# A macaron layer: scanning in place in PSUM, expert parameters in one tensor of two halves, and parts of setup and plan moved into the first units

## The chip, the cores and the metric

The kernel runs on one core of one Trainium2 chip, in float32. The metric is the time of one execution on the device in microseconds. A core has five engines with instruction queues of their own: PE (matrix products), DVE (vector), ACT (activation functions), POOL (which also issues the indirect gathers and scatters) and SP (which issues the direct transfers). Each engine works through its queue in order; semaphores order them among one another. The products of PE land in PSUM, eight banks of 128 x 512 floats.

## The reference

```
x = x + 0.5 * moe(layernorm(x))
x = x + block(layernorm(x))
x = x + 0.5 * moe(layernorm(x))
```

There are 4096 tokens (2 sequences of 2048) of 256 features. `moe` gives each token its two best of 8 experts by a softmax gate. Each expert takes at most 640 tokens of first and 640 of second choices, in token order; what comes later is dropped. Expert: `relu(x @ W1 + b1) @ W2 + b2` with 1024 hidden features, times the gate's probability.

`block` is a selective scan followed by a small MLP, each behind an RMS norm. Its core, for 512 channels and 16 states:

```
u  = silu(causal_conv4(x @ in_proj))         # and a gate z
dt = softplus(low_rank(u) @ dt_proj + b)
h[t] = h[t-1] * exp(dt[t] * A) + dt[t] * u[t] * B[t]     # per channel and state
y[t] = sum over states (h[t] * C[t]) + D * u[t]
out  = (y * silu(z)) @ out_proj
```

Then comes `x + relu(norm(x) @ c_fc)^2 @ c_proj`. The inputs are seeded random numbers; the gate's and the experts' biases are small random numbers.

## The kernel before, in words

**Routing.** `setup` makes constants and loads the block's weights; on DVE it builds `half`, sixteen diagonal matrices `taps` (a convolution tap on the diagonal, so that PE does the convolution) and four `skip`, and scales `w_out`. `moe1` then routes the 32 tiles of 128 tokens in groups of 4, 4, 8, 8 and 8 (`route`): layer norm, gate logits, top two, position of each token in its expert's list. `store_list` puts the lists into DRAM.

**Plan.** The tokens of an expert are cut into units of 256 rows. `plan` (L643) works out on DVE, from the counts, which expert and which rows each possible unit has, for 39 units at once; `fetches` and `index` turn this into row numbers for the gathers. In the first MoE the units of the first half of the tokens come first and then those of the second half, so `plan` gets 16 columns, 8 experts for each half.

**First MoE.** `run_units` runs 22 units (`NU_A`) through `units` (L762): for unit u, ids of u+5 are gathered, `hidden` multiplies by W1 (PE, ACT), the rows of u+1 are transposed, `finish` multiplies by W2, adds the bias on DVE and issues two scatter-adds into `acc` in DRAM on POOL, and then the rows and parameters of u+3 are gathered into one of three buffers. A unit whose expert's parameters are in that buffer already gets a row number out of range, so that its gather moves nothing; the instruction remains. An expert's parameters are two gathers: 8,224 bytes a partition from `expert_in` (W1, b1) and 9,216 from `expert_out` (W2, b2). `then` is a table of functions that are called at the start of a unit: `begin_rest` at unit 18 asks for the ids and parameters of the first spread unit.

**The block.** The tokens are cut into eight chunks of 512. The scan's loop (`recurrence`) has 512 slots: 8 chunks x 4 channel blocks x 16 states. In a slot POOL makes `db` = dt·u·B, ACT makes `dA` = exp(dt·A) into PSUM (`decay`), DVE runs the scan along the 512 tokens into another PSUM bank `h`, ACT copies the last column as the state (`st`), DVE multiplies by C into `hc`, and PE adds `hc` up in `y_ps`. The pools `dA` and `h` have two banks each, `ps` and `yps` too. In the loop `scan(k)` and its `st` copy come ahead of `decay(k + 2)`:

```
            if k < len(order):
                scan(k)
                decay(k + 2)
            if k:
                output(k - 1)
            drive(k + 3)
```

**What is placed between the slots.** Everything else of the block, and 21 more units of the two MoEs, is cut into steps that the class `Side` puts between the slots when the program is built. Ten "b" units (`NU_B`) belong to the first MoE (second half of the tokens), eleven "c" units (`NU_C`) to the second (first half); `spread_units` builds both, with one parameter buffer in two parts, `wa` and `wb`. `chunk_front` prepares a chunk (norm, projection, convolution, `dt`, B and C), `chunk_tail` finishes it (output projection, MLP, and the routing for the second MoE). `Side` keeps a book of each engine's time. A slot adds `OWN` to it (DVE 1.95, ACT 0.88, POOL 1.27 us), a step adds its own cost, and a step is placed when its engines are not further ahead of the slot than `BEHIND` allows. If the loop needs a result that is not placed yet (`side.until`: for example `dt` of the next chunk, or the previous chunk's output before `gate`), the steps up to it are all placed at once at that slot. Which engine runs what in which order is thus fixed by this book, whose times are not measured during the run.

**Second MoE.** During the block, the lists are planned a second time (`plan_half` after four chunks, `plan_rest` after the last); then 21 units (`NU_D`) run as in the first MoE, added to `out`.

Of the kernel before, what the change touches and what calls it, by code (L numbers as in the profile page):

```python
# [18 lines left out]
P = 128  # L19
# [23 lines left out]
W_2 = W_B1 + NF  # L43
W_B2 = W_2 + NF * D
WW = W_B2 + D

# [29 lines left out]
class Side:  # L76
# [6 lines left out]
    OWN = {"dve": 1.95, "act": 0.88, "pe": 0.0, "pool": 1.27}  # L83
# [101 lines left out]
class Feed:  # L185


    def __init__(self, kernel, todo, data, pool, pre="", nids=8, nrows=4):
        self.nc, self.pool, self.pre = kernel.nc, pool, pre
        self.expert = kernel.ins["expert_in"], kernel.ins["expert_out"]  # L190
        self.idx, _, self.widx = todo
        self.lists, self.rows, _ = data
        self.nids, self.nrows = nids, nrows
        self.ids, self.xb = {}, {}
# [26 lines left out]
    def params_of(self, u, to):  # L221

        n = to.shape[1]
        parts = [to] if n < WW else [to[:, :W_2], to[:, W_2:]]
        for a in parts:
            src = self.expert[a.shape[1] != W_2]
            self.gather(a, src, self.widx[:, u : u + 1], E * P - 1)


class Kernel:  # L230
# [6 lines left out]
    def setup(self):  # L237
# [4 lines left out]
        self.wa = self.keep.tile([P, W_2], F32, tag="wa", name="wa")  # L242
        self.wb = self.keep.tile([P, WW - W_2], F32, tag="wb", name="wb")
        dp = self.ctx.enter_context(self.tc.tile_pool(name="scratch", bufs=1, space=DRAM))

        def const(shape, name, dtype=F32):
            return cp.tile(shape, dtype, tag=name, name=name)

        self.ident = const([P, P], "ident")
        make_identity(nc, self.ident)  # L250
        self.ones = const([P, P], "ones")
        nc.gpsimd.memset(self.ones, 1.0)

        self.before = const([P, P], "before")
        nc.gpsimd.affine_select(
            out=self.before, in_=self.ones, pattern=[[1, P]], compare_op=ALU.is_gt,
# [32 lines left out]
        self.before_b, self.ones_b = const([P, P], "before_b", BF16), const([P, P], "ones_b", BF16)  # L289
        nc.vector.tensor_copy(self.before_b, self.before)  # L290
        nc.vector.tensor_copy(self.ones_b, self.ones)
# [24 lines left out]
        nc.sync.dma_start(out=self.gb, in_=ins["gate_b"].partition_broadcast(P))  # L316
        def weights(name, src, k, n):
            t = const([P, k, n], name)
            nc.sync.dma_start(out=t, in_=ins[src].rearrange("(k p) n -> p k n", p=P))
            return t  # L320
# [23 lines left out]
        for c in range(NC):  # L344
# [7 lines left out]
        a_log = const([P, NC, DS], "a_log")  # L352
        nc.sync.dma_start(out=a_log, in_=ins["A_log"].rearrange("(c p) s -> p c s", p=P))
        a_exp = const([P, NC, DS], "a_exp")
        nc.scalar.activation(a_exp, a_log, AF.Exp)
        self.A = const([P, NC, DS], "A")
        nc.vector.tensor_scalar_mul(self.A, a_exp, -1.0)

        sizes = (NT, NT, NT // 2)
        self.rows = [
            dp.tile([n + 1, RW], F32, tag=f"rows{i}", name="rows") for i, n in enumerate(sizes)
        ]
        self.lists = [dp.tile([NULL + 1, 1], I32, tag=f"list{i}", name="lists") for i in range(3)]
        with self.tc.tile_pool(name="once", bufs=1) as once:
            row = once.tile([1, RW], F32, tag="none", name="none")
            nc.gpsimd.memset(row, 0.0)
            for t, n in zip(self.rows, sizes):
                nc.sync.dma_start(out=t[n:, :], in_=row)  # L370
            for i, n in enumerate((NT, NT // 2, NT)):
                none = once.tile([1, 1], I32, tag=f"none{i}", name="none")
                nc.gpsimd.memset(none, n)
                nc.sync.dma_start(out=self.lists[i][NULL:, :], in_=none)
        self.acc = dp.tile([NT, D], F32, tag="acc", name="acc")

# [266 lines left out]
    def plan(self, t, M, kept, half, nu, off, size=MU):  # L643
# [6 lines left out]
        V = nu.shape[1]  # L650
        WV, WE, WB = [P, M, V], [P, M, E], [P, M, UB]
        cu, cx, cb = t("cu", [P, V]), t("cx", [P, V]), t("cb", [P, V])
        v.tensor_tensor_scan(cu, self.ones[:, :V], nu, 0.0, ALU.mult, ALU.add)
# [11 lines left out]
        if V > E:  # L665
            ie = t("ie", WE)
            v.tensor_tensor(ie, inn[:, :, :E], inn[:, :, E:], ALU.add)
            inn = ie
# [48 lines left out]
    def fetches(self, t, name, eu, nwb, known=0):  # L717
# [3 lines left out]
        same, at, widx = t("same", [P, n]), t("at2", [P, n]), t(name, [P, n], I32)  # L721
# [4 lines left out]
        v.scalar_tensor_tensor(at, eu, float(P), self.part[:, :n], ALU.mult, ALU.add)  # L726
        v.scalar_tensor_tensor(widx, same, SKIP, at, ALU.mult, ALU.add)
        return widx
# [9 lines left out]
    def first_expert(self, pool):  # L738

        w = pool.tile([P, WW], F32, tag="w0", name="w0")  # L740
        self.nc.sync.dma_start(out=w[:, :W_2], in_=self.ins["expert_in"][:P, :])
        self.nc.sync.dma_start(out=w[:, W_2:], in_=self.ins["expert_out"][:P, :])
        return w
# [4 lines left out]
    def parts(self, *w):  # L748

        a, b = w[0][:, :W_2], w[-1][:, -(WW - W_2) :]  # L750
        return (
            a[:, :W_B1].rearrange("p (k f) -> p k f", k=ND), a[:, W_B1:],
            b[:, : W_B2 - W_2].rearrange("p (f d) -> p f d", f=NF), b[:, W_B2 - W_2 :],
        )
# [93 lines left out]
    def bank(self, lone):  # L848

        if not lone:  # L850
            return self.mm, "mm"
        self.lent += 1
        self.spare = self.spare[1:] + self.spare[:1]
        return self.spare[-1]

    def spread_units(self, feed, m0, acc, last, pool, name, slots, known):
# [4 lines left out]
        wa, wb = self.wa, self.wb  # L861
        w1, b1, w2, b2 = self.parts(wa, wb)
        if not known:
# [3 lines left out]
            feed.params_of(0, wa)  # L867
# [3 lines left out]
            feed.params_of(0, wb)  # L871
# [33 lines left out]
        for u, slot in enumerate(slots):  # L905
# [25 lines left out]
            if u + 1 < n:  # L931
                yield Need(pool=1.0, sets=(name + "wa", u + 1), late=9.0)
                feed.params_of(u + 1, wa)
# [13 lines left out]
            if u + 1 < n:  # L947
                yield Need(pool=1.0, sets=(name + "wb", u + 1), late=9.0)
                feed.params_of(u + 1, wb)

    def scratch(self, pool):
        def t(name, shape, dtype=F32):
            return pool.tile(shape, dtype, tag=f"p_{name}", name=name)

        return t
# [11 lines left out]
    def moe1(self):  # L967
# [4 lines left out]
        with ExitStack() as ctx:  # L972
# [27 lines left out]
            with tc.tile_pool(name="m1_lps", bufs=1, space=PSUM) as ps:  # L1000
# [4 lines left out]
            tot, off = t("tot", [P, K2, E]), t("off", [P, K2 * E])  # L1005
            v.tensor_tensor(tot[:, 0, :], half[:, :E], half[:, E:], ALU.add)
            v.tensor_tensor(tot[:, 1, :], kept[:, :E], kept[:, E:], ALU.add)
            nu = self.need(t, tot.rearrange("p c e -> p (c e)"), "nu")
            v.tensor_tensor(nu[:, E:], nu[:, E:], nu[:, :E], ALU.subtract)
            v.tensor_scalar_mul(off[:, :E], nu[:, :E], 0.0)  # L1010
            v.tensor_copy(off[:, E:], nu[:, :E])
            at, m0, eu, cu, _ = yield_from(self.plan(t, MU, kept, half, nu, off))


            over, o2, ok = t("over", [P, 1]), t("o2", [P, 1]), t("ok", [P, 1])
            v.tensor_scalar_add(over, cu[:, E - 1 : E], -float(NU_A))
            v.tensor_scalar_add(o2, cu[:, K2 * E - 1 :], -float(NU_A + NU_B))
            v.tensor_tensor(over, over, o2, ALU.max)
            v.tensor_scalar_max(over, over, 0.0)
            v.tensor_scalar(ok, over, 0.0, None, ALU.is_equal)  # L1020
            more = t("more_i", [P, 1], I32)
            v.tensor_copy(more, over)
            todo = self.index(t, "idx", at), m0, self.fetches(t, "widx", eu, NWB, 1)
            rest = slice(NU_A, NU_A + NU_B)
            m0b = keep("m0b", [P, NU_B, UB])
            v.tensor_copy(m0b, m0[:, rest, :])
            self.rest = (
                self.index(keep, "idxb", at[:, rest, :], ok), m0b,
                self.fetches(keep, "widxb", eu[:, rest], 1),
            )  # L1030
            data = self.lists[0], self.rows[0], self.acc
            self.feed_b = Feed(self, self.rest, data, self.keep, "e_", 4, 2)

            def begin_rest():
                self.feed_b.ids_of(0)
                self.feed_b.params_of(0, self.wa)
                self.feed_b.params_of(0, self.wb)

            then = {NU_A - 4: begin_rest, NU_A - 2: lambda: self.feed_b.rows_of(0)}
            self.run_units("m1", NU_A, todo, more, w, data, Feed(self, todo, data, pool), pool, then)  # L1040

# [17 lines left out]
    def plan_half(self, pool):  # L1059
# [14 lines left out]
        done, d2 = keep("done", [P, E]), t("d2", [P, E])  # L1074
        v.tensor_scalar(d2, cx, -1.0, float(NU_C), ALU.mult, ALU.add)
        v.tensor_scalar_max(d2, d2, 0.0)
        v.tensor_tensor(done, d2, nu, ALU.min)
# [3 lines left out]
        self.todo = self.index(keep, "idxc", at), m0c, self.fetches(keep, "widxc", eu, 1)  # L1081
# [251 lines left out]
    def recurrence(self, pools, chunks, side):  # L1333
# [36 lines left out]
        def decay(k):  # L1370
            if k < len(order):
                i, c, s = order[k]
                dA[k] = pools["dA"].tile(W1, F32, tag="dA", name="dA")
# [4 lines left out]
        def scan(k):  # L1378
            i, c, s = order[k]
            ch = chunks[i]  # L1380
            if k % (NC * DS) == 0:
                ch["state"] = stp.tile([P, NC, DS], F32, tag="st", name="st")
            h[k] = pools["h"].tile(W1, F32, tag="h", name="h")
            nc.vector.tensor_tensor_scan(  # L1384
                h[k], dA.pop(k), db.pop(k),
# [132 lines left out]
    def mamba(self):  # L1518
# [3 lines left out]
        with ExitStack() as ctx:  # L1522
# [5 lines left out]
            def aside(name, bufs):  # L1528
# [11 lines left out]
                "dA": pool("dA", 2, space=PSUM),  # L1540
                "h": pool("h", 2, space=PSUM),
# [3 lines left out]
            self.spare = [(pools["dA"], "dA"), (pools["h"], "h")]  # L1545
# [51 lines left out]
def layouts(inputs):  # L1597
# [9 lines left out]
        ff["b1"].reshape(E, NF, P).transpose(0, 2, 1),  # L1607
        ff["W2"].reshape(E, NF, P, D).transpose(0, 2, 1, 3).reshape(E, P, NF * D),
        np.broadcast_to(ff["b2"][:, None, :], (E, P, D)),
# [13 lines left out]
        "expert_in": np.concatenate(per_expert[:2], 2).reshape(E * P, W_2),  # L1623
        "expert_out": np.concatenate(per_expert[2:], 2).reshape(E * P, WW - W_2),
    }
# [18 lines left out]
```

## Time and profile before

| | |
|---|---|
| three runs | 2423.73, 2425.97, 2438.62 us (median 2425.97) |
| the profiled run | 2435.03 us, of it span 2433.3 us |
| PE busy | 2063.3 us, 85% |
| POOL busy | 1520.0 us, 62% |
| DVE busy | 1342.2 us, 55% |
| ACT busy | 1028.3 us, 42% |
| granted PE clock | 0.933 of full speed, mean |
| DMA | 328.51 MB, 135 GB/s mean |

The page's slices over the span (each of 40 is 60.8 us; a digit is the busy share in tenths) show the stages:

```profile
PE   5399999597988888896888887798997988699996
...
DVE  6611111115877868499788788785887823211111
ACT  3122222126546557455466663764663532122211
POOL 2366555429787768486577774885786742655553
```

Routing and plan are the first two slices, the first MoE the next six, with little DVE; then the block's front, the scan loop from about 572 to 1961 us, its tail, and the second MoE from about 2085 us. In the later views a row reads: line, engine, operation, out<-in by the program's names, shapes, count; busy time and mean duration in ns of one; the idle time ahead of it and what ended most of that. In a timeline a row begins with its start and its duration, and in brackets stands the idle time ahead of it.

### The profile page before, as it was taken

The page shows a single profiled execution, that of the slowest core. Times are in us where ns is not written, and L with a number is a line of the kernel's source. Part 1 is how long each engine was busy: PE and PEld are TensorE (multiplying, and loading weights), DVE is VectorE, ACT ScalarE, POOL GpSimd, SP SyncE. Part 2 cuts the span into 40 slices and gives each one's busy share as a digit, 9 for nine tenths or more (in the row PEclk, how much of TensorE's full clock was granted, in tenths as well). Part 3 has the DMA queues.
Part 4 walks back from the last instruction along what each step waited for, and adds up shares of the span by engine and source line. Part 5 has one row for each costly group of instructions (what it writes and reads, how often), then busy time and mean ns, then how long its engine had stood idle before and what let it go on. Part 6 is the DMA issues. An engine that isn't in the chain of part 4 may idle for free. (4 is left out here: it accounts for less than half of the span.)

```text
span 2433.3 us, 24340 instructions
## 1 busy us (share of the span) xinstructions
PE 2063.3 (85%) x7253; PEld 1317.4 (54%) x7253; DVE 1342.2 (55%) x2234; ACT 1028.3 (42%) x2335; POOL 1520.0 (62%) x1481
## 2 busy tenths in 40 slices
PE   5399999597988888896888887798997988699996
PEld 1188878453544454553433333354545566588875
DVE  6611111115877868499788788785887823211111
ACT  3122222126546557455466663764663532122211
POOL 2366555429787768486577774885786742655553
PEclk8699999798999999998999999999998999899998
DMA  7165556323655546364345354465455632455553
GB/s 248 58 207 147 173 162 210 81 62 84 169 136 128 120 128 162 90 169 113 97 113 147 100 143 98 124 190 126 99 132 137 150 117 67 118 165 178 177 180 98
DMA packets 163693, 328.51 MB, mean 135 GB/s; under 512 B 31795, under 2 KB 78748, under 8 KB 149212
## 3 DMA queue, kind: packets, MB, share of 16 engines
q1 hardware_dynamic: 116156, 173.92, 27.9%
q0 software_dynamic: 47392, 152.90, 21.7%
q8 instruction: 61, 1.00, 0.2%
q14 instruction: 84, 0.69, 0.1%
HBM read 316.35 MB, written 36.38 MB: 145 GB/s over the span
## 5 line engine op out<-in xcount | busy, mean ns | idle before, releaser
L1368 POOL TENSOR_TENSOR db<-dtu,bt 128x512 f32<-128x512 f32 x512 | 653.0, 1321 | 190.8 <-DVE h L1384 90.5
L1405 PE MATMUL y_ps<-hc,ident 128*128 128x512 f32 x1024 | 546.7, 636 | 120.7 <-DVE hc L1394 119.5
L1384 DVE TENSOR_TENSOR_SCAN h<-dA,st,db 128x512 f32<-128x512 f32 x384 | 494.5, 1288 | 73.0 <-POOL db L1368 35.7
L1405 PEld LDWEIGHTS y_ps<-hc,ident 128*128 128x128 f32 x1024 | 186.0, 197 | 369.3 <-DVE hc L1394 243.0
L794 ACT ACTIVATE h<-hp,w 128x256 f32<-128x256 f32 x344 | 144.4, 471 | 564.6 <-PE hp L836 473.5
L1374 ACT ACTIVATE dA<-dt,A 128x512 f32<-128x512 f32 x512 | 358.4, 700 | 2.5 <-POOL dt L1294 2.3
L1394 DVE TENSOR_TENSOR hc<-h,ct 128x512 f32<-128x512 f32 x512 | 344.7, 673 | 15.7 <-ACT st L1389 15.4
L836 PE MATMUL hp<-xbT,w 128*128 128x256 f32 x1376 | 308.0, 382 | 12.3 <-issue 11.5
L843 PE MATMUL yp<-w,h 128*128 128x256 f32 x1376 | 307.6, 382 | 0.0
L836 PEld LDWEIGHTS hp<-xbT,w 128*128 128x128 f32 x1376 | 264.0, 192 | 49.6 <-issue 11.9
L843 PEld LDWEIGHTS yp<-w,h 128*128 128x128 f32 x1376 | 260.9, 192 | 34.5
L1389 ACT COPY st<-h 128x1 f32<-128x1 f32 x512 | 81.2, 159 | 388.0 <-DVE h L1384 386.1
L779 DVE COPY xbT<-tp 128x512 f32<-128x512 f32 x43 | 29.7, 691 | 344.4 <-PE tp L775 344.4
L836 PE MATMUL e_hp<-e_xT,wa 128*128 128x256 f32 x672 | 180.8, 419 | 15.2 <-DVE h L1384 7.1
L1384 DVE TENSOR_TENSOR_SCAN h<-dA,db 128x512 f32<-128x512 f32 x128 | 157.2, 1228 | 51.0 <-POOL db L1368 38.9
L836 PEld LDWEIGHTS e_hp<-e_xT,wa 128*128 128x128 f32 x672 | 141.0, 213 | 70.6 <-issue 27.7
L805 DVE TENSOR_TENSOR y<-yp,w 128x256 f32<-128x256 f32 x86 | 36.5, 424 | 238.7 <-PE yp L843 238.7
L197 POOL DMA_INDIRECT xb<-rows,ids x128 | 134.3, 1049 | 37.6 <-issue 33.7
L843 PE MATMUL e_yp<-wb,e_h 128*128 128x256 f32 x672 | 152.9, 382 | 1.0 <-DVE xc L1213 1.0
L843 PEld LDWEIGHTS e_yp<-wb,e_h 128*128 128x128 f32 x672 | 128.6, 192 | 29.8 <-issue 10.8
L757 POOL DMA_INDIRECT acc<-y,ids x44 | 70.1, 1594 | 108.7 <-DMA acc<-y,ids 52.6
L757 POOL DMA_INDIRECT out<-y,ids x42 | 66.7, 1589 | 105.1 <-DMA out<-y,ids 65.7
(313 smaller groups left out, 2584.1 us busy)
## 6 DMA issues: line engine op xcount, KB each, us to landing
bt<-bc SPq DMA_DIRECT2D x256, 256.0 KB, 3.9
ct<-bc SPq DMA_DIRECT2D x256, 256.0 KB, 4.5
rows<-row SPq DMA_DIRECT2D x12, 512.0 KB, 4.7
x<-in_x SPq DMA_DIRECT2D x8, 512.0 KB, 4.5
acc<-x SPq DMA_DIRECT2D x8, 512.0 KB, 5.1
xt<-acc SPq DMA_DIRECT2D x8, 512.0 KB, 5.5
x<-acc SPq DMA_DIRECT2D x8, 512.0 KB, 4.8
out<-xt SPq DMA_DIRECT2D x8, 512.0 KB, 4.8
```

The costliest lines, as they stand in the source:

```text
L197: self.nc.gpsimd.indirect_dma_start(out=out, out_offset=None, in_=src, in_offset=bass.IndirectOffsetOnAxis(ap=idx, axis=0), bounds_check=l ...
L757: self.nc.gpsimd.indirect_dma_start(out=dst, out_offset=bass.IndirectOffsetOnAxis(ap=ids, axis=0), in_=y, in_offset=None, bounds_check=las ...
L794: nc.scalar.activation(h[:, f + q, :], hp[:, q, :], AF.Relu, bias=b1[:, f + q : f + q + 1])
L805: nc.vector.tensor_tensor(y[:, j, :], yp, b2, ALU.add)
L836: self.nc.tensor.matmul(hp[:, q, :], lhsT=w1[:, k, (f + q) * P : (f + q + 1) * P], rhs=xT[:, k, :], start=(k == 0), stop=(k == ND - 1),)
L843: self.nc.tensor.matmul(yp, lhsT=h[:, f, j * P : (j + 1) * P], rhs=w2[:, f, :], start=(f == 0), stop=(f == NF - 1),)
L1368: nc.gpsimd.tensor_tensor(db[k], chunks[i]["dtu"][c // PR][:, q, :], bt[n], ALU.mult)
L1374: nc.scalar.activation(dA[k], chunks[i]["dt"][c], AF.Exp, scale=self.A[:, c, s : s + 1])
L1384: nc.vector.tensor_tensor_scan(h[k], dA.pop(k), db.pop(k), chunks[i - 1]["state"][:, c, s : s + 1] if i % (T // TC) else 0.0, ALU.mult, AL ...
L1389: nc.scalar.copy(ch["state"][:, c, s : s + 1], h[k][:, TC - 1 :])
L1394: nc.vector.tensor_tensor(t, h.pop(k), ct[k // PR], ALU.mult)
L1405: nc.tensor.matmul(y[c], lhsT=self.ident, rhs=hc.pop(k), start=False, stop=(s == DS - 1))
```

## The change

The change has five parts.

- **Scan in place.** `dA` and `h` become one pool `h` of four PSUM banks. `decay` writes a bank of it, and the scan writes its result over its own `dA`.
- **One tensor of parameters.** `expert_in` and `expert_out` become `expert`, with rows of 4,608 floats in two halves: W1, b1 and padding; b2 and W2. A whole unit takes one gather of 18,432 bytes a partition. The spread units take a half at a time through a view with two rows per expert, with an index of their own (`halves`); `wa` and `wb` are one tile `w`.
- **Block weights beside the first units.** The block's weights, `taps`, `skip`, `w_out`'s scale and `A` move from `setup` into `setup_block`, called at unit 1. `before_b` and `ones_b` are made directly, without a cast.
- **Plan in two.** `now` holds the first MoE's units but ten of the second half, `late` those ten. `plan` works on 8 columns. The late ten are planned in a function at unit 12, and `begin_late` stands at unit 18 where `begin_rest` stood.
- **Planner.** `OWN` of DVE is 1.8 in place of 1.95.

The diff, cut to its core:

```diff
+WH = NF * D + D
+WW = 2 * WH
...
-    OWN = {"dve": 1.95, "act": 0.88, "pe": 0.0, "pool": 1.27}
+    OWN = {"dve": 1.8, "act": 0.88, "pe": 0.0, "pool": 1.27}
...
     def params_of(self, u, to):
-        n = to.shape[1]
-        parts = [to] if n < WW else [to[:, :W_2], to[:, W_2:]]
-        for a in parts:
-            src = self.expert[a.shape[1] != W_2]
-            self.gather(a, src, self.widx[:, u : u + 1], E * P - 1)
+        self.gather(to, self.expert, self.widx[:, u : u + 1], E * P - 1)
+
+    def half_of(self, u, w, i):
+        src = self.expert.rearrange("e (h c) -> (e h) c", h=2)
+        self.gather(w[:, i * WH : (i + 1) * WH], src, self.widx[:, u, i : i + 1], 2 * E * P - 1)
...
             nu = self.need(t, tot.rearrange("p c e -> p (c e)"), "nu")
-            v.tensor_tensor(nu[:, E:], nu[:, E:], nu[:, :E], ALU.subtract)
-            v.tensor_scalar_mul(off[:, :E], nu[:, :E], 0.0)
-            v.tensor_copy(off[:, E:], nu[:, :E])
-            at, m0, eu, cu, _ = yield_from(self.plan(t, MU, kept, half, nu, off))
+            late, now = keep("late", [P, E]), keep("now", [P, E])
+            v.tensor_tensor(late, nu[:, E:], nu[:, :E], ALU.subtract)
+            self.first_of(t, late, late, NU_B)
+            v.tensor_tensor(now, nu[:, E:], late, ALU.subtract)
+            v.tensor_scalar_mul(off, now, 0.0)
+            at, m0, eu, cu, _ = yield_from(self.plan(t, MU, kept, half, now, off))
...
+            def plan_late():
+                s = self.scratch(pool, "q")
+                at, m0, eu, _, _ = yield_from(self.plan(s, NU_B, kept, half, late, now))
+                m0b = keep("m0b", [P, NU_B, UB])
+                v.tensor_copy(m0b, m0)
+                self.rest = self.index(keep, "idxb", at), m0b, self.halves(keep, "widxb", eu)
+                self.feed_b = Feed(self, self.rest, data, self.keep, "e_", 4, 2)
+
+            def begin_late():
+                self.feed_b.ids_of(0)
+                for i in range(2):
+                    self.feed_b.half_of(0, self.w, i)
...
+            then = {
+                1: self.setup_block, NU_A - 10: plan_late, NU_A - 4: begin_late,
+                NU_A - 2: lambda: self.feed_b.rows_of(0),
+            }
...
-                dA[k] = pools["dA"].tile(W1, F32, tag="dA", name="dA")
+                dA[k] = pools["h"].tile(W1, F32, tag="h", name="h")
...
-            h[k] = pools["h"].tile(W1, F32, tag="h", name="h")
+            h[k] = dA.pop(k)
             nc.vector.tensor_tensor_scan(
-                h[k], dA.pop(k), db.pop(k),
+                h[k], h[k], db.pop(k),
...
-                "dA": pool("dA", 2, space=PSUM),
-                "h": pool("h", 2, space=PSUM),
+                "h": pool("h", 4, space=PSUM),
```

`setup_block` holds the lines taken out of `setup` unchanged, but for `A`, which ACT now makes in two operations (exponential, times -1) in place of one on ACT and one on DVE.

## The prediction

> **What bounds the kernel now.** I read the profile from the outside in: the busy time of each engine by stage, then the costliest groups, then the rows of the stage that a part of the change touches. The stages, cut at 87, 112, 459, 572, 1961 and 2085 us, are routing, plan, first MoE, front of the block, scan loop, tail, second MoE (columns: busy time and count of PE, PEld, DVE, ACT, POOL; clock; DMA share):
>
> ```profile
> 0.00:87.00 87.00, 42.01 (x202) 17.96 (x202) 61.06 (x278) 31.63 (x63) 22.13 (x61) 0.79 0.63 206
> 87.00:112.00 25.00, 0.57 (x4) 0.14 (x1) 15.69 (x63) 0.00 (x0) 6.45 (x7) 0.50 0.03 7
> 112.00:459.00 347.00, 324.96 (x1496) 280.39 (x1496) 54.74 (x153) 73.90 (x176) 201.75 (x175) 0.97 0.57 169
> ...
> 572.00:1961.00 1389.00, 1213.04 (x3471) 631.18 (x3471) 1107.26 (x1443) 777.80 (x1774) 1002.20 (x957) 0.95 0.51 129
> ```
>
> Routing and plan hang on DVE, the MoE stages on PE (94% busy) with POOL close, and the loop on DVE and PE in turns, 80% and 87% busy. The page's groups give the price of a slot of the loop:
>
> ```profile
> L1368 POOL TENSOR_TENSOR db<-dtu,bt 128x512 f32<-128x512 f32 x512 | 653.0, 1321 | 190.8 <-DVE h L1384 90.5
> ...
> L1384 DVE TENSOR_TENSOR_SCAN h<-dA,st,db 128x512 f32<-128x512 f32 x384 | 494.5, 1288 | 73.0 <-POOL db L1368 35.7
> ...
> L1374 ACT ACTIVATE dA<-dt,A 128x512 f32<-128x512 f32 x512 | 358.4, 700 | 2.5 <-POOL dt L1294 2.3
> L1394 DVE TENSOR_TENSOR hc<-h,ct 128x512 f32<-128x512 f32 x512 | 344.7, 673 | 15.7 <-ACT st L1389 15.4
> ```
>
> DVE's scan and product are 1.288 + 0.673 = 1.96 us; 512 of them are about 1000 of the loop's 1389 us. ACT waited 2.5 us in all before `dA`: the two-buffer pools do not hold anyone up.
>
> **The scan in place.** The scan reads `dA` from PSUM already and writes PSUM already; now both are one bank. Nothing is freed sooner: ACT's own order (copy of `st` for slot k ahead of the decay of k+2) stays, and that copy waits for scan k. So the four buffers buy at most the 2.5 us above; I take 0. The duration in place is not in the trace. The near rows are ACT's:
>
> ```profile
> L1207 ACT ACTIVATE cv_ps<-cv_ps,half 128x512 f32<-128x512 f32 x32 | 21.0, 657 | 60.2 <-PE cv_ps L1200 60.1
> L1270 ACT ACTIVATE dt_ps<-dt_ps,chan 128x512 f32<-128x512 f32 x32 | 20.9, 654 | 0.0
> ```
>
> In place in a bank they take 654 and 657 ns; out of a bank into SBUF ACT takes 681 (with a bias, into `dtu`) or 596 (`th`, without). The ratios, 0.96 and 1.10, bound the scan at 1.24 and 1.42 us. The Trainium skill speaks against sharing a bank ("PSUM — Partial Sum Buffer", section "PSUM bank collisions raise a hardware error"): each bank is a RAM of its own, and two engines must not be in it together. Here one engine is, and the page prices that nowhere; by its one-RAM remark the upper end would be right, by the rows, with PE accumulating in place at full rate (636 ns), no change. I take 1.288. Each 0.1 us is 51 us of DVE, times its 80% share.
>
> **The planner's slot (1.95 to 1.8).** This moves side work, and its PE pieces stand between two `y_ps` products. I priced those gaps in the built order with PE's rows as they run back to back (four of 512 columns 1.88 us, sixteen of 256 3.62). Pieces above 5 us, slot and us, before: 125: 15.1, 160: 22.0, 224: 11.2, 288: 6.0, 352: 11.8, 416: 16.8, 480: 13.0; after: 125: 14.7, 160: 11.2, 189: 8.6, 224: 9.1, 251–253: 14.6, 352: 6.0, 381: 10.8, 416: 27.6, 480: 15.1. The scans of before do stand still there: 35.1 us between two at slot 160, 24.3 at 416, 17.7 at 352, 17.2 at 224, 7.4 at 288, 5.0 at 253. Scaling each by its own piece: 160 -18, 352 -9, 288 -5, 224 -1 (-33), and 416 +12, 480 +3, 251–253 +13, 189 +5, 381 +5 (+38). One C unit's PE work, 10.8 us, leaves the loop for the tail: about -5 in the loop, where half of it lies beside DVE, and +3 in the tail (bounds 0 and +8). Loop: 0, with 25 either way, since a forced mark need not cost what its neighbour did.
>
> **Routing.** The block weights' DVE work leaves this row of setup:
>
> ```profile
> 31.16 3.21 DVE L339 TENSOR_SCALAR taps<-ident,half 128x128 f32<-128x128 f32 x16
> ```
>
> With `half` 0.62, `skip` 0.93, `A` 0.18 and two casts 0.44 it is 5.4 us in a chain in which PE waits for DVE; part overlaps, I take -4.7 (bounds -5.4 and -2). It is done again in unit 1, where DVE has 4.2 us of its own in 14.25 of PE: hidden, 5 us if that cover is gone. Of its DMAs, eight issues of SP (8 us) go behind the first row stores, still ahead of the later ones, and land long before unit 1. ACT does two small operations more there: 0.
>
> **Plan.** With 8 columns for 16, five operations on 624 elements (0.80 us) become 312 elements (about 0.48): -1.6; `ie` -0.47; the second half's index operations -0.75; seven small operations new, +0.8. I take -2.0. The late half, some 48 small operations of 0.2 us, joins unit 12: 10 us, with DVE's 4.2 the same as PE's 14.25, so +1 (bounds 0 and +3). Behind it in DVE's queue are `xbT` and `y`, on which PE and then POOL's scatter wait.
>
> **One gather per expert.** POOL's timeline of one unit:
>
> ```profile
> 149.84 1.62 POOL L757 DMA_INDIRECT acc<-y,ids  x1 [0.30 <-issue]
> 155.20 1.56 POOL L757 DMA_INDIRECT acc<-y,ids  x1 [3.73 <-DMA acc<-y,ids]
> 157.06 1.07 POOL L197 DMA_INDIRECT xb<-rows,ids  x1 [0.31 <-PE yp L843]
> 158.43 1.05 POOL L197 DMA_INDIRECT xb<-rows,ids  x1 [0.30 <-issue]
> 159.78 0.99 POOL L197 DMA_INDIRECT w<-in_expert_in,widx  x1 [0.30 <-issue]
> 161.08 1.00 POOL L197 DMA_INDIRECT w<-in_expert_out,widx  x1 [0.30 <-issue]
> ```
>
> The cycle to the next first scatter (164.99) is 15.15 us against PE's 14.25. The new kernel drops one issue, 1.30 us. But the scatter's landing stands in the same queue behind the parameters: 3.73 us here, 3.04 after a unit that loads nothing (repeated expert). The Trainium skill ("DMA: Bandwidth & Descriptors", section "Anatomy of one DMA — SWDGE (gpsimd) path") gives a DMA 2.0 us plus bytes over 436 kB/us: two transfers of 1.05 and 1.18 MB would be 9.1 us, one of 2.36 MB 7.4, a clear gain. In the trace the two overlap: the second lands 9.5 us after the first's issue, bytes flowing without a break. So the issue saved goes mostly into the wait: between -1.3 (landing follows issue) and +0.35 (0.13 MB more at some 400 kB/us, the rate at which the two transfers moved between 147 and 152.7 us); near the row, -0.3. POOL bounds 11 units of the first MoE (transposes of 252.52 to 433.33, 24.1 us over 11 times 14.25) and 10 of the second (2236.15 to 2392.72, 14.1 over): -3.3 and -3.0. At the first MoE's start three issues fewer give POOL a lead of 3.9; hidden(1) then waits for a whole row of 2.36 MB (+0.9): -3.0. At the second's, the last C unit's second half is now asked for only after the plan, in POOL's queue behind ids and rows: hidden(0) stood 21.8 us behind the plan's end, waiting for an empty repeated gather, and I keep that with +1 (bounds 0 and +7.3, the whole delay of that half).
>
> **Sum** on the profiled run, 2435.03 us (span 2433.3): routing -4.7, plan -2.0, first MoE -3.0 - 3.3 + 1.0, loop 0, tail +3.0, second MoE -3.0 + 1.0: -11.0, so 2424. The median of the runs is 2425.97, 0.9963 of that run: 2415.
>
> **The rivals.** *POOL falls under PE and the scan is shorter.* If each saved issue counts whole, both MoE stages go to 14.25 us a unit (-17 with the lead, -14), and at 1.24 us the scan gives 0.05 x 512 x 0.8 = -20: -4.7 - 2 - 17 + 1 - 20 + 3 - 13 = -53, 2373. For it: the plain arithmetic of POOL; against it: the wait that shrinks with an empty queue. *The planner's piles take over.* A shorter slot in its books makes side chains last more slots, until `dt` of chunk 4 is forced at slot 251 and 27.6 us of PE stand at 416. If the four relieved piles give nothing, since their work only moves to places where PE, 87% busy, is waited for as well, the loop is +33, and with the late half of the last C unit +6.3: +28, or 2454. It decides once those piles return less than 28 of the 33 us. For it: PE's share; against it: the 35.1 us gap is real, and its pile is halved. *The scan in place is slow,* 1.42 us: 0.13 x 512 x 0.8 = +53, so 2468; only ACT's 1.10 speaks for it. *The change does not do what it says:* four buffers free nothing earlier. That is in my sum at 0.
>
> **How the numbers follow.** About what a measurement can tell from no change is 1%, 24 us. Likeliest case 0.48, 2415, its own range 2390 to 2438; gain 0.29, 2373; piles 0.15, 2454; slow scan 0.08, 2468. Faster by over 1%: nearly all of the gain and a fifth of the likeliest, 0.38; slower: the slow scan and most of the piles, 0.17; the rest 0.45. The range runs from 2372 to 2453, which leaves out the slow scan and the ends of the others.
>
> **What would show it.** Scan rows at 1.23 to 1.29 us; gaps of the scans near 17 us at slot 160, near 36 at 416, and new ones at 251 and 381; first ids of POOL near 97 us rather than 103.72; a POOL cycle with a load near 14.9 us, its scatter's wait 4.7 rather than 3.7; moe units still at 14.25 before POOL binds. Wrong would be: a scan row off by 0.05 us, a POOL cycle at 14.25, or a loop whose length leaves 1389 by over 25 us.

## The result, and the profile after

The changed kernel takes 2398.24 us (median, 2397.45 to 2398.59), the kernel before 2425.27 in the same series: ratio 0.9876, interval 0.9841 to 0.9911. Forecast were 2415 us and 2372 to 2453. On another chip the same two kernels gave 0.988 (0.9855 to 0.9904).

Of the profiled runs, span 2433.3 and 2396.8 us, here is where the time went. The boundaries are DVE's copies of transposed rows (`xbT`) and the first and last scan; the run before was itself some 10 us above its median, so the sum here is 36.5 and not 27.

| stage | before | after | difference | forecast |
|---|---|---|---|---|
| start to unit 1 | 124.9 | 121.0 | -3.9 | -9.7 with routing, plan, POOL's lead |
| rest of the first MoE's units | 311.1 | 306.6 | -4.5 | -2.3 |
| last units, front of the block | 134.3 | 132.7 | -1.6 | 0 |
| loop, first to last scan | 1384.0 | 1354.9 | **-29.1** | 0, with 25 either way |
| tail to unit 1 of the second MoE | 154.2 | 158.5 | +4.3 | +4.0 |
| second MoE's units | 286.5 | 289.2 | +2.7 | -3.0 to the end |
| last unit's end | 38.3 | 33.9 | -4.4 | |

So four fifths of the difference lie in the loop, where the prediction had zero. The loop of before is known from this one trace alone, of a run above its median, so its 29.1 us may be several too many. The page's groups after (busy us, mean ns, idle ahead of it) show no reason: the scan and the product cost what they did.

```profile
L1380 POOL TENSOR_TENSOR db<-dtu,bt 128x512 f32<-128x512 f32 x512 | 653.0, 1315 | 189.0 <-DVE h L1396 107.9
...
L1396 DVE TENSOR_TENSOR_SCAN h<-h,st,db 128x512 f32<-128x512 f32 x384 | 491.6, 1280 | 46.5 <-POOL db L1380 37.5
...
L1406 DVE TENSOR_TENSOR hc<-h,ct 128x512 f32<-128x512 f32 x512 | 344.4, 673 | 31.4 <-ACT st L1401 31.3
L1386 ACT ACTIVATE h<-dt,A 128x512 f32<-128x512 f32 x512 | 358.5, 701 | 3.8 <-POOL dt L1306 3.4
```

The scan is 1280 ns in place of 1288. What changed is when each starts. DVE's timeline (start, duration) for two slots back to back, first of the kernel before:

```profile
970.63 0.67 DVE L1394 TENSOR_TENSOR hc<-h,ct 128x512 f32<-128x512 f32 x1
971.43 1.29 DVE L1384 TENSOR_TENSOR_SCAN h<-dA,st,db 128x512 f32<-128x512 f32 x1
972.63 0.67 DVE L1394 TENSOR_TENSOR hc<-h,ct 128x512 f32<-128x512 f32 x1
973.44 1.29 DVE L1384 TENSOR_TENSOR_SCAN h<-dA,st,db 128x512 f32<-128x512 f32 x1
```

and then of the changed one:

```profile
998.98 0.67 DVE L1406 TENSOR_TENSOR hc<-h,ct 128x512 f32<-128x512 f32 x1
999.57 1.27 DVE L1396 TENSOR_TENSOR_SCAN h<-h,st,db 128x512 f32<-128x512 f32 x1
1000.76 0.67 DVE L1406 TENSOR_TENSOR hc<-h,ct 128x512 f32<-128x512 f32 x1
1001.35 1.28 DVE L1396 TENSOR_TENSOR_SCAN h<-h,st,db 128x512 f32<-128x512 f32 x1
```

From the start of a product to the start of the next scan it was 0.80 us, 0.13 more than the product lasts; now it is 0.59, 0.08 less. The step from scan to product is 1.20 and 1.19. A slot back to back took 2.00 us and takes 1.78. The waits of the scan, counted in the two built programs, name the cause:

```
before: 446 of 512 scans wait for  DVE, ACT, POOL
after:  468 of 512 scans wait for       ACT, POOL
```

The order on DVE is scan(k), hc(k-1), scan(k+1). Before, scan(k+1) writes the `h` bank that hc(k-1) reads, and in 342 of the 512 scans that is the instruction just ahead (in the others, side work stands between). So it waits until its own neighbour has finished altogether; otherwise the two overlap by 0.08 us. It is not the count of waits that changed: 510 scans before and 468 after have one waiting instruction ahead of them, and only before is DVE among those waited for. In place, scan(k+1) writes where `dA` lay, and that bank's last reader on DVE is known to be done when ACT writes `dA`. Call this theory W, the own wait. Its rival, theory P, is that the loop gained by the planner's new placing.

### The profile page after: what moved, and what is told of

It is laid out like the page before. It is cut to its first block, busy times and chain, and to the rows that moved or that the text cites. A ratio compares the mean times of both kernels' runs of the same rounds, so it can differ in the third digit from the quotient of the medians.

```text
span 2396.8 us, 24185 instructions
## 1 busy us (share of the span) xinstructions
PE 2048.8 (85%) x7253; PEld 1306.8 (55%) x7253; DVE 1332.1 (56%) x2271; ACT 1026.5 (43%) x2336; POOL 1476.6 (62%) x1438
## 5 line engine op out<-in xcount | busy, mean ns | idle before, releaser
L1396 DVE TENSOR_TENSOR_SCAN h<-h,st,db 128x512 f32<-128x512 f32 x384 | 491.6, 1280 | 46.5 <-POOL db L1380 37.5
L1386 ACT ACTIVATE h<-dt,A 128x512 f32<-128x512 f32 x512 | 358.5, 701 | 3.8 <-POOL dt L1306 3.4
L842 PE MATMUL e_hp<-e_xT,w 128*128 128x256 f32 x672 | 167.3, 397 | 18.1 <-DVE e_y L948 8.0
L1396 DVE TENSOR_TENSOR_SCAN h<-h,db 128x512 f32<-128x512 f32 x128 | 156.3, 1221 | 44.6 <-POOL db L1380 41.1
L842 PEld LDWEIGHTS e_hp<-e_xT,w 128*128 128x128 f32 x672 | 133.4, 201 | 62.5 <-issue 19.2
L811 DVE TENSOR_TENSOR y<-yp,w 128x256 f32<-128x256 f32 x86 | 36.5, 424 | 235.4 <-PE yp L849 235.4
L849 PE MATMUL e_yp<-w,e_h 128*128 128x256 f32 x672 | 155.4, 386 | 8.7 <-DMA w<-in_expert,widxc 8.4
L849 PEld LDWEIGHTS e_yp<-w,e_h 128*128 128x128 f32 x672 | 129.1, 193 | 42.2 <-issue 23.2
```

What stands on the lines that cost most here:

```text
L811: nc.vector.tensor_tensor(y[:, j, :], yp, b2, ALU.add)
L842: self.nc.tensor.matmul(hp[:, q, :], lhsT=w1[:, k, (f + q) * P : (f + q + 1) * P], rhs=xT[:, k, :], start=(k == 0), stop=(k == ND - 1),)
L849: self.nc.tensor.matmul(yp, lhsT=h[:, f, j * P : (j + 1) * P], rhs=w2[:, f, :], start=(f == 0), stop=(f == NF - 1),)
L1386: nc.scalar.activation(dA[k], chunks[i]["dt"][c], AF.Exp, scale=self.A[:, c, s : s + 1])
L1396: nc.vector.tensor_tensor_scan(h[k], h[k], db.pop(k), chunks[i - 1]["state"][:, c, s : s + 1] if i % (T // TC) else 0.0, ALU.mult, ALU.add,)
```

## The experiments

Ratios are to the kernel before on the same chip, which lay between 2425 and 2443 us from chip to chip.

**1. Two pools again.** The scan alone is put back.

```diff
...
-                dA[k] = pools["h"].tile(W1, F32, tag="h", name="h")
+                dA[k] = pools["dA"].tile(W1, F32, tag="dA", name="dA")
...
-            h[k] = dA.pop(k)
+            h[k] = pools["h"].tile(W1, F32, tag="h", name="h")
             nc.vector.tensor_tensor_scan(
-                h[k], h[k], db.pop(k),
+                h[k], dA.pop(k), db.pop(k),
...
-                "h": pool("h", 4, space=PSUM),
+                "dA": pool("dA", 2, space=PSUM),
+                "h": pool("h", 2, space=PSUM),
```

> The changed kernel with the scan alone put back: dA and h in pools of two banks each, everything else (planner's 1.8, one gather, moved setup) as changed. Theory W (own wait): a scan that writes a bank of its own must wait until the product just ahead of it in DVE's queue has finished with that bank; in place it needs not. Start to start of two scans back to back then returns from 1.78 to 2.00 us, the scan row stays at 1.28, and with some 270 such slots the loop grows by 45 to 60 us: about 2445 us. Theory P (planner): the loop's gain comes from where the side work is placed, which is the same here: 2398 us, within 8.

2428.69 us, ratio 0.9951 (0.9935 to 0.9967) against the changed kernel's 0.988. The spacing is back at 2.00 us (DVE's timeline of this run; 1106.92 less 1104.91):

```profile
1104.91 1.29 DVE L1397 TENSOR_TENSOR_SCAN h<-dA,st,db 128x512 f32<-128x512 f32 x1
1106.12 0.67 DVE L1407 TENSOR_TENSOR hc<-h,ct 128x512 f32<-128x512 f32 x1
1106.92 1.29 DVE L1397 TENSOR_TENSOR_SCAN h<-dA,st,db 128x512 f32<-128x512 f32 x1
```

W has its mechanism, but not its size: 45 to 60 us more in the loop were expected. It takes 1369.4 us: 14.5 more than the changed kernel's 1354.9, and 11.7 more than the 1357.7 of run 4, which has the changed kernel's loop and ran on this chip. The changed kernel has 270 slots closer than 1.9 us; at 0.22 each they are worth 59. In the slots that take 2.1 to 7 us, where DVE waits for somebody, the time over 1.94 us a slot is 230 us with two pools and 264 to 272 in place (changed kernel, run 4). So 34 to 42 us are given back there, and 5 to 12 more in the longest gaps: DVE comes sooner to the same waits. In the loop those of the scan for POOL's `db` rise from 65.0 us with two pools to 78.6 in the changed kernel, those of DVE for PE's results from 86 to 98.

**2. The planner's 1.95 in the changed kernel.**

```diff
-    OWN = {"dve": 1.8, "act": 0.88, "pe": 0.0, "pool": 1.27}
+    OWN = {"dve": 1.95, "act": 0.88, "pe": 0.0, "pool": 1.27}
```

> The changed kernel with the planner's DVE time of a slot back at 1.95. Theory W: the spacing of scans back to back stays at 1.78 us, and the time moves by what the places of the side work are worth, under 20 us either way: 2380 to 2418 us. Theory P: the loop's gain of 29 us is lost: about 2427 us. The prediction had put the two placings within 25 us of each other.

Ratio 0.9878 (0.9852 to 0.9904), the changed kernel's own. The spacing stays at 1.78, the loop is 1368.2 us. P fails as an account of the whole gain: the number is worth nothing in the end. But the loop by itself is longer, by 10.5 us against run 4 on the same chip and by 13.3 against the first trace, so P holds for that part of it; experiment 11 shows where it goes.

**3. The scan in place in the kernel before,** the same edit the other way round, with the planner's 1.95.

> The kernel before with the scan in place alone (four banks of one pool), planner's 1.95 and all the rest as before. Theory W: spacing 1.78 instead of 2.00 us in some 270 slots, so 30 to 55 us less, 2370 to 2395 us. Theory P, and the prediction's own zero for the scan: 2425 us, within 8.

Ratio 0.9958 (0.9942 to 0.9973), 10 us: less than theory W's 30 to 55, and not the zero of the other side either. The spacing is 1.78 us, the loop 1368.7, 15.3 less than in the trace of before, which is of another chip: again about a quarter of what the spacing promises. On the chip of runs 1 to 4 alone, the loop is 11.7 us shorter in place (1369.4 less 1357.7) and 10.5 shorter by the placing (1368.2 less 1357.7). That is 22 us of the loop's 29. The other 7 are no more than what the trace of before, some 10 us over its median, and the chips leave open: the changed kernel's loop took 1348.5 to 1357.7 us in the traces of the result and of runs 4 to 7 and 10.

**4. POOL's order in the whole units.** Ids and rows of later units are asked for between a unit's two scatters.

```diff
                 self.scatter_add(acc[:, :], ids[u][:, j : j + 1], y[:, j, :], NT - 1)
+                if j == 0:
+                    between()
...
-            fetch_ids(u + 5)
             h = hidden(u)
             transpose(u + 1)
-            finish(u, h)
-            fetch(u + NWB)
+            def between():
+                fetch_ids(u + 5)
+                if u + NWB < hi:
+                    feed.rows_of(u + NWB)
+            finish(u, h, between)
+            if u + NWB < hi:
+                feed.params_of(u + NWB, w[(u + NWB) % NWB])
```

> The changed kernel, in the whole units of both MoEs with the ids and the rows of later units asked for between a unit's two scatters, so that POOL's wait for the first scatter's landing (4.9 us) is covered by four issues (5.2 us). If that wait is what makes POOL's cycle 15.1 us against PE's 14.25, all units run at 14.25: -19 in the first MoE, -16 in the second: about 2364 us. If the queue's data is the limit (the landing moves back with the gathers put ahead of it), 2398 us within 8.

2361.32 us, ratio 0.9658 (0.9629 to 0.9688): from unit 2 on, the first MoE's units stand 14.2 or 14.3 us apart, but for the one with the late plan (15.2) and the next (13.3), and so do the second's, but for an early pair (15.3 and 13.2). In all that is some 54 us less than the changed kernel's ratio (46 in run 10), where 34 was expected. POOL's timeline of one unit of the changed kernel, then of this one:

```profile
148.01 1.57 POOL L763 DMA_INDIRECT acc<-y,ids  x1 [5.71 <-DMA acc<-y,ids]
149.88 1.07 POOL L196 DMA_INDIRECT xb<-rows,ids  x1 [0.31 <-issue]
151.26 1.03 POOL L196 DMA_INDIRECT xb<-rows,ids  x1 [0.30 <-issue]
152.59 0.99 POOL L196 DMA_INDIRECT w<-in_expert,widx  x1 [0.30 <-issue]
...
156.50 1.63 POOL L763 DMA_INDIRECT acc<-y,ids  x1 [0.31 <-issue]
163.01 1.57 POOL L763 DMA_INDIRECT acc<-y,ids  x1 [4.88 <-DMA acc<-y,ids]
```

```profile
172.80 1.60 POOL L763 DMA_INDIRECT acc<-y,ids  x1 [4.10 <-DVE y L812]
174.71 1.04 POOL L196 DMA_INDIRECT ids<-lists,idx  x1 [0.31 <-issue]
...
178.68 1.00 POOL L196 DMA_INDIRECT xb<-rows,ids  x1 [0.30 <-issue]
179.99 1.64 POOL L763 DMA_INDIRECT acc<-y,ids  x1 [0.30 <-issue]
181.93 1.04 POOL L196 DMA_INDIRECT w<-in_expert,widx  x1 [0.31 <-issue]
187.06 1.59 POOL L763 DMA_INDIRECT acc<-y,ids  x1 [4.08 <-DVE y L812]
```

The changed kernel's cycle is 15.0 us, 4.9 of it waiting for a scatter's landing behind the parameters in the queue. In the new order the second scatter follows without a wait, and POOL waits 4.1 us a unit for DVE: it has slack.

**5. The changed kernel again,** on the chip of the next three.

> The changed kernel once more, beside the runs that follow, since the chip of the last four had a kernel before of 2442 rather than 2425 us. Ratio to the kernel before 0.984 to 0.991 as on the first chip; scans back to back 1.78 us apart.

2400.89 us, ratio 0.988 (0.9855 to 0.9904); spacing 1.78 us, loop 1351.7.

**6. Two gathers.** The same bytes, from two tensors.

```diff
...
-        self.gather(to, self.expert, self.widx[:, u : u + 1], E * P - 1)
+        for a, src in ((to[:, :WH], self.expert_a), (to[:, WH:], self.expert_b)):
+            self.gather(a, src, self.widx[:, u : u + 1], E * P - 1)
```

> The changed kernel with the whole units' parameters in two gathers again (two halves of 9,216 bytes a partition, the same bytes). The prediction's queue reading (the issue saved is waited for instead): POOL's cycle in units with a load stays at 15.1 us, and only the start costs more (up to 4 us of POOL's lead): +3 to +8 us in all. The plain count (1.30 us for each of 21 units in which POOL binds): +27 us.

Ratio 0.9937 (0.9917 to 0.9957) against 0.988: 14 us, between the two expectations. The first MoE's units from unit 1 are no further apart, 310.4 us against 310.8; the second's take 294.0 against 291.4. The rest is at the edges, +3.4 in the tail and +3.6 after the last unit, where PE is done and POOL works off what it is behind. The two profiled runs differ by 9.8 us; where the rest of the 14 lies they do not show.

**7. The block's weights in the setup again.**

```diff
+        self.setup_block()
...
-                1: self.setup_block, NU_A - 10: plan_late, NU_A - 4: begin_late,
+                NU_A - 10: plan_late, NU_A - 4: begin_late,
```

> The changed kernel with the block's weights made in the setup again. The prediction: routing 4.7 us later, unit 1 unchanged: +4.7 us (bounds +2 and +5.4). If the move was worth nothing (routing bound by something else, or unit 1 pays): 0.

Ratio 0.9897 (0.9875 to 0.9919): 4 us by the ratios, 2.3 by the medians, and the intervals overlap, so the gain is not clear of noise. The first ids are gathered at 104.71 us in place of 100.95.

**8. The scan over `db` in SBUF.**

```diff
...
-            h[k] = dA.pop(k)
+            h[k] = db.pop(k)
             nc.vector.tensor_tensor_scan(
-                h[k], h[k], db.pop(k),
+                h[k], dA.pop(k), h[k],
...
```

> The changed kernel with the scan writing over its other operand, db in SBUF, instead of dA in PSUM (five buffers of db, four of hc; dA keeps four PSUM banks). Theory W: what counts is only that the scan writes no place that the product ahead of it reads, so the spacing of scans back to back is 1.78 us or less here too. If it is the reading and writing of one PSUM bank that makes it quick, the spacing goes back to 2.00 us. The product reads SBUF here, which may move its own 0.67 us; total 2380 to 2430 us by theory W, no sharper since POOL's db now waits for the product.

2577.7 us, ratio 1.0611 (1.0582 to 1.0639), far outside what was expected, for a reason of its own. DVE and POOL in the timeline of this run:

```profile
999.76 0.66 DVE L1406 TENSOR_TENSOR hc<-db,ct 128x512 f32<-128x512 f32 x1
...
1001.34 2.50 POOL L1380 TENSOR_TENSOR db<-dtu,bt 128x512 f32<-128x512 f32 x2
...
1002.57 1.83 DVE L1406 TENSOR_TENSOR hc<-db,ct 128x512 f32<-128x512 f32 x1
...
1004.58 1.27 POOL L1380 TENSOR_TENSOR db<-dtu,bt 128x512 f32<-128x512 f32 x1 [0.73 <-DVE hc L1406]
1005.52 0.87 DVE L1406 TENSOR_TENSOR hc<-db,ct 128x512 f32<-128x512 f32 x1
...
1006.32 1.27 DVE L1396 TENSOR_TENSOR_SCAN db<-dA,st,db 128x512 f32<-128x512 f32 x1
```

The product now reads both operands from SBUF, and its mean rises from 673 to 1104 ns: it hardly gets on while POOL's product runs. POOL's pair ends at 1003.84, 1.27 us after this product began, which lasts 1.83; the next has 0.33 us of POOL beside it and lasts 0.87; the one at 999.76, with none, lasts 0.66. The question put is answered all the same: the scan at 1006.32 begins 0.07 us ahead of the product's end. There is no gap, so the gain does not come from PSUM. The slow product is what the Trainium skill states ("SBUF — State Buffer", section "SBUF: two separate sides"): DVE with two SBUF inputs and a reading POOL share a pair of ports, held for a whole instruction. This run agrees: 1.27 us of waiting beside 0.56 of work.

**9. The product at once,** straight behind the scan that it reads.

```diff
                 scan(k)
+                output(k)
                 decay(k + 2)
-            if k:
-                output(k - 1)
```

> The changed kernel with the order of two instructions on DVE turned: the product hc of slot k comes straight behind the scan of slot k, whose result it reads, instead of behind that of slot k+1. Banks, row durations and all other work stay. Theory W in its general form (an instruction that needs the one just ahead of it on its own engine starts about 0.2 us later than one that needs not): the spacing of scans back to back goes from 1.78 back to 2.00 us, the gap now ahead of the product, and the time rises by 10 to 25 us, as with two pools. If the 0.2 us belonged to writing a bank that was just read: 1.78 us and 2400 us within 8 of the changed kernel's.

2543.06 us, ratio 1.0483. This tells nothing of W, since the order brought in another wait: the product also waits for ACT's one-column copy out of the same bank. The group's row:

```profile
L1406 DVE TENSOR_TENSOR hc<-h,ct 128x512 f32<-128x512 f32 x512 | 354.2, 692 | 229.4 <-ACT st L1401 229.4
```

The spacing is 2.12 us. It does show what the distance of one slot between scan and product is good for: it hides `st`.

**10 to 12. POOL's new order at three numbers of the planner.** The edit of 4 with `OWN` at 1.8, 1.95 and 1.7.

> The order of POOL between the two scatters once more, as the base of the next two on this chip: ratio to the kernel before 0.962 to 0.970, units at 14.25 us.

> POOL's new order with the planner's 1.95. The runs so far show 1.8 worth 10 to 14 us in the loop and costing 7 to 11 behind it (one C unit more in the tail, a later start of the second MoE): same as the run before within 8 us. If the placing matters by itself, off by 15 us or more.

> POOL's new order with the planner's 1.7, below the 1.78 us that a slot takes at its quickest. If the planner's number works by matching the slot, 1.7 is no better than 1.8 (within 8 us, or worse by up to 20 since more work is left to forced places and to the tail); if smaller is simply better, 10 us less.

| `OWN` of DVE | time | ratio | loop | after the loop |
|---|---|---|---|---|
| 1.8 | 2352.22 | 0.9691 (0.9671 to 0.9711) | 1352.2 | 463.8 |
| 1.95 | 2354.60 | 0.9702 (0.9683 to 0.9722) | 1358.7 | 455.7 |
| 1.7 | 2372.87 | 0.9779 (0.9759 to 0.9800) | 1386.4 | 448.7 |

From 1.95 to 1.8 the loop is 6.5 us shorter and what follows it 8.1 longer. At 1.7 the gaps of the scans at slots 250 to 254 alone are 58 us: work left to the forced mark of chunk 4. Smaller is not better. The order of 4 and 10, with 1.8, is the quickest found, though 1.95 cannot be told from it: 3.1 to 3.4% below the kernel before, 2% below the changed one.

## Why the prediction was right or wrong

The time lies in the range, and in the likeliest case's own; the point is 17 us high. That the range held is in part luck: it was wide because of the loop, whose 25 us either way were meant for the side work, and the scan's gain fell into that. The loop of the profiled runs is 29 us shorter, and a loop off by over 25 is what the prediction itself had named as a sign of being wrong. Taken one at a time, the parts are worth 10 to 17 us (scan in place, runs 1 and 3), 14 (one gather, run 6), 2 to 4 (block weights, run 7) and about 0 (planner, runs 2 and 11), together some 26 to 35 against the 27 to 29 measured. By its steps:

**The scan in place: wrong.** The step that failed is "Nothing is freed sooner ... So the four buffers buy at most the 2.5 us above; I take 0." It looked at who waits for a buffer across engines, and found right that ACT does not. It did not look at the scan's wait for its own engine. The row durations held (1.280; forecast 1.288, bounds 1.24 and 1.42), so the one-RAM remark of the Trainium skill has no price here, but the start-to-start times of 2.00 us stood in the trace of before against 1.288 + 0.673 = 1.96 with nobody named for the gap. Runs 1 and 3 show what comes of it: 10 to 17 us where the prediction had zero.

**The planner: right at the end, by two errors.** Forecast were loop 0 and +4 behind it; measured are -7 and -11 within one chip, +5 to +8 behind it, and zero within the noise in all (runs 2 and 11). The piles went as worked out where they were relieved, even further: the gap at slot 160 fell from 35.1 to 11.8 us (forecast 17), at 352 from 17.7 to 6.0. At 416 the gap is 40.2; forecast were 36, but the prediction's own rule gives 24.3 x 27.6 / 16.8 = 40 (and at 224 a fall of 3, not 1; measured is 13.9 us, 3.3 less). The new gaps are larger: 19.4, 10.6 and 8.9 at 252, 254 and 259, where 18 in all was forecast. DVE waits there 7.5 us for a load (`x<-acc`), and 7.5 and 4.6 for ACT's `st`, so a forced place costs more than the matmul rows say. The gap near slot 125, 20.6 us before, is not among the prediction's gaps; it rose to 26.3, though PE's piece there was to stay as it is (15.1 and 14.7). The rival of the piles was thus half right. Its loop comes true at 1.7: 1386.4 us, 34 above that at 1.8.

**Routing and plan: right, too large.** First ids at 99.55 us, not 97: -4.2 instead of -6.7. Routing gave 3.4 of 4.7 (the counts' sum `tot` went from 87.60 to 84.23), in run 7 3.8. The plan gave 0.8 of 2.0, since the "seven small operations new, +0.8" were mis-sized. They hang on one another. DVE's timeline of the plan after:

```profile
84.69 0.16 DVE L667 COPY X<-half 128x8 f32<-128x8 f32 x1
84.77 0.16 DVE L668 TENSOR_TENSOR X<-half 128x8 f32<-128x8 f32 x1
...
86.07 0.17 DVE L1052 TENSOR_SCALAR left<-sums 128x8 f32<-128x8 f32 x1
86.28 0.17 DVE L1053 TENSOR_SCALAR left<-left 128x8 f32<-128x8 f32 x1
86.48 0.17 DVE L1054 TENSOR_TENSOR late<-left,late 128x8 f32<-128x8 f32 x1
86.68 0.17 DVE L1018 TENSOR_TENSOR now<-nu,late 128x8 f32<-128x8 f32 x1
```

Independent neighbours start 0.08 us apart, those that need each other 0.20, at the same length. That is theory W once more, in another stage. It is the nearest neighbour that counts: `sums<-ones,late` at 85.65 in the same plan needs `late` from 85.42, has two others in between, and starts 0.08 us behind the last of them. The Trainium skill ("VectorE: DVE Perf Modes", section "The DRAIN you can't avoid") says that chaining operations on DVE without semaphores gains nothing, for the next waits until the pipe is empty anyway, though it adds that one which is not held starts earlier. By the former the prediction's 0 would have been right; these rows and runs 1 and 3 side with the latter: what waits for nothing starts earlier.

**One gather: right in the units, wrong on where the gain lies.** The cycle is 15.0 us (forecast 14.9), the wait 4.9 (4.7): the issue saved is waited for. In the first MoE's units nothing beyond noise came of the "-0.3"; the plain count of the issue would have shown as 1.3 us a unit, the prediction's 9.1 against 7.4 as 1.7, and neither did. In all one gather gains 14 us in run 6, where 9.3 was forecast. But the 3.0 of POOL's lead at the first MoE's start are not there: unit 1 begins at 121.26 us with two gathers and at 121.57 with one. What POOL is ahead shows late, in the tail, the second MoE and after the last unit. The rival that both MoE stages fall to 14.25 us a unit needed another edit, run 4.

**Units 1 and 12: right.** In run 10, where POOL does not bind, the unit with the late plan takes 15.2 us and the next 13.3: the +1 is taken back at once. Unit 1 shows nothing.

## What to carry to other kernels

An instruction that waits for the one just ahead of it on its own engine does not show as idle time with a cause: look at start-to-start times of back-to-back slots and compare them with a pair that is independent. Write where no neighbour has just read. When a saving falls on an engine that shares the bound (here DVE at 80% with PE at 87%), do not count all of it: here 10 to 17 of 59 us came through. And when a wait for a landing sits in an engine's queue, put other issues between before making issues fewer: that was worth 46 to 54 us more, against 27 to 29 for the whole change.

## What was not expected of the hardware

- On DVE a wait for the instruction just ahead costs 0.1 to 0.2 us in start-to-start time: 0.80 against 0.59 behind a 0.67 us product, 0.20 against 0.08 among operations of 0.17.
- How dear two SBUF operands are on DVE beside a busy POOL: the product's mean is 1104 ns against 673 with one operand in PSUM, single ones 1.83 us against 0.66, and the kernel 6% slower than before. With the scan's result in PSUM it is out of POOL's way.
- The changed kernel kept its ratio from chip to chip, but the kernels did not keep their time: the kernel before had medians of 2425, 2443, 2432 and 2429 us. On the chip of 2443 (runs 1 to 4) the first two units of the first MoE stood 16.6 to 20.8 us apart, on the others 10.0 to 11.1; why is open.
